# The last token tile of a cross-attention and FFN kernel in smaller pieces, with new order constants

## The chip, the cores and the metric

The kernel runs on one core of a Trainium2 chip. Its time is the device time of one execution in microseconds, and the figure used is the median over runs. A core has five engines with queues of their own: TensorE (PE, matmuls; its weight loads are shown as PEld), VectorE (DVE), ScalarE (ACT), GpSimd (POOL) and SyncE (SP, which here only issues transfers). Each queue is worked off in the order in which the program wrote it.

## The reference

There are 8 batches of 100 tokens with 512 features, and for each a context of 722 rows. Sixteen heads of 32 features attend to the context with sparsemax in place of softmax. The FFN multiplies the normalized tokens with the cosine of one matrix and the sine of another, and takes the length of the two results.

```python
def sparsemax(x):
    x = x - jnp.max(x, axis=-1, keepdims=True)
    zs = -jnp.sort(-x, axis=-1)
    rho = jnp.arange(1, L + 1, dtype=x.dtype)
    cssv = jnp.cumsum(zs, axis=-1) - 1.0
    k = jnp.maximum(jnp.sum(zs > cssv / rho, axis=-1, keepdims=True), 1)
    tau = jnp.take_along_axis(cssv, k - 1, axis=-1) / k.astype(x.dtype)
    return jnp.clip(x - tau, 0.0)

h = layernorm(x)                                     # x: (8, 100, 512)
scores = heads(h @ Wq + bq) @ heads(ctx @ Wk + bk).T * 32 ** -0.5
out = sparsemax(scores) @ heads(ctx @ Wv + bv)
x = x + merge(out) @ Wo + bo
h = layernorm(x)
real = h @ cos(theta + theta_noise)
imag = h @ sin(phi + phi_noise)
return x + sqrt(real * real + imag * imag)
```

All numbers are fp32.

## The kernel before

**Tiles.** The 800 tokens are cut into seven tiles (`TILES`: six of 128 rows and one of 32). The attention works by batch, eight of them. A tile's norm and queries come before the batches it belongs to; its last steps (output product, residual, second norm, FFN, result) follow when the last of its batches has its outputs. Tile 6, the last, holds rows 672 to 799 and so ends with batch 7; tile 5 ends with batch 6.

**A batch.** TensorE makes keys (`keys`, L559; for batch 0 also `keys_part`, L548) and values (`values`, L581) from the context. It makes the scores in ten fills of a PSUM tile of four banks, `psc` (`fill`, L606 and L617); ScalarE copies each to SBUF (`fill_copy`, L628); VectorE takes the eight largest of each stretch of some 30 scores (`tops`, L639). From these candidates the threshold of sparsemax is found in five Newton steps (`above`, `above_values`, `above_count`, `update`; L706 to L732), on VectorE with a product on POOL. POOL cuts the threshold into three bf16 parts (`parts`, L747 to L764), TensorE transposes them (`parts_T`, L769), ScalarE copies them. Then, in five groups of up to five pairs of head group and context chunk (`PAIRS`): TensorE makes the scores again less the threshold (`weights`, L813 and L826) in `psc`, ScalarE takes the relu (`weights_relu`, L838), TensorE multiplies with the values (`outputs`, L849), and after the last chunk of a head group ScalarE adds the bias into a quarter of `oT` (`outputs_bias`, L863). There is one `psc` and one `aT` buffer, so the next weights wait for the relu before, and other PE work is put between. For the last batch the threshold search is cut into three ranges of rows.

**Last steps of a tile** (`last_steps`): `product` (L502) multiplies the four quarters of `oT` with Wo; `residual` (L511) adds on VectorE; `stats`, `deviation`, `normed` (L443 to L455), `normed_T` (L463) and `normed_copy` (L469) are the norm; two more products (L502) with the cosine and sine matrices; `square` on ScalarE (L515), `square_sum` on POOL (L518), `root` on ScalarE (L521), `result` on POOL (L525), which also issues the store from POOL's queue (L526).

**The order.** No loop writes the program. Every step is a task with an engine and an assumed cost (`STEPS`), its forerunners, and the buffers it takes and frees (`hold`). `Plan.order` gives each engine, whenever it is free, the ready task that can start first, and among several the one with the smallest due time:

```python
t.due = t.batch * PERIOD - t.rank + LAG.get(t.kind, 0.0)
...
stay = STAY if engine == "PE" and t.shape == shape else 0.0
key = (max(start, now + WINDOW), t.due - stay)
```

`rank` is the longest path of costs to the end, `LAG` a constant for each kind of task, and `STAY` favours PE work of the same tiling as the work before it. A ready task is never left in order to wait for a more urgent one that isn't ready. The order found is what each engine's queue holds.

**The check.** After the planned part, VectorE reduces what `keep_checks` (L739, L740) recorded to one flag (L1190 to L1203, with a transpose on TensorE, L1199). All engines read it (L1204), and a slow general path runs if it is set; for these inputs it is not.

Of the kernel before, what the change touches and what calls it, by code (L numbers as in the profile page):

```python
# [11 lines left out]
FP = mybir.dt.float32  # L12
# [10 lines left out]
P = 128  # L23
# [12 lines left out]
FS = 16  # L36
# [7 lines left out]
def fills_of(left_first):  # L44
# [52 lines left out]
    "load ctx": ("SP", 4.8),  # L97
    "load w": ("SP", 0.8),
    "load bias": ("SP", 0.1),
    "stats": ("DVE", 0.85),  # L100
    "deviation": ("ACT", 0.25),
    "normed": ("DVE", 0.65),
# [28 lines left out]
    "values": ("PE", 3.43),  # L131
    "values copy": ("ACT", 0.55),
    "weights": ("PE", 0.05, 0.25),
    "weights relu": ("ACT", 0.12, 0.335),
    "outputs": ("PE", 0.0, 0.184),
    "outputs bias": ("ACT", 0.05, 0.28),
# [5 lines left out]
    "square sum": ("POOL", 1.25),  # L142
    "root": ("ACT", 0.6),
    "result": ("POOL", 1.9),
    "turns": ("POOL", 3.5),
    "turned": ("POOL", 2.05),
    "bounded": ("POOL", 0.7),
# [3 lines left out]

SHAPE = {"fill": 1, "fill last": 2, "outputs": 2, "weights": 3}
CHANGE = (0.19, 0.1, 0.1, 0.1)
STAY = 175.0
PERIOD = 121.0
WINDOW = 0.0
LAG = {
    "above": 260.0,
    "above count": -180.0,
    "above values": -150.0,  # L160
    "add bo": -5.0,
    "bounded": -75.0,
    "candidates": -190.0,
    "checks": 30.0,
    "deviation": 165.0,
    "ffn": 300.0,
    "fill": -240.0,
    "fill copy": 30.0,
    "fill last": -235.0,
    "first bound": 270.0,  # L170
    "keys": -65.0,
    "keys bias": 280.0,
    "keys part": -285.0,
    "leftovers": 250.0,
    "load bias": 205.0,
    "load ctx": 295.0,
    "load part": 120.0,
    "load w": 200.0,
    "load x": -160.0,
    "load x again": 180.0,  # L180
    "losses": 250.0,
    "normed": -80.0,
    "normed 2": -110.0,
    "normed T": -65.0,
    "normed copy": -245.0,
    "output product": 235.0,
    "outputs": -205.0,
    "outputs bias": 70.0,
    "parts": -180.0,
    "parts T": -165.0,  # L190
    "parts copy": -240.0,
    "parts copy last": -285.0,
    "queries": -285.0,
    "queries bias": -215.0,
    "residual": -55.0,
    "rests": 130.0,
    "result": 150.0,
    "sines": -300.0,
    "square": -215.0,
    "square sum": 275.0,  # L200
    "stats": 100.0,
    "stats 2": 265.0,
    "tops": 240.0,
    "turned": 160.0,
    "turns": -255.0,
    "update": 55.0,
    "update far": 155.0,
    "values": 110.0,
    "values copy": -200.0,
    "weights": -80.0,  # L210
    "weights relu": 300.0,
}


# [13 lines left out]
class Plan:  # L228
# [9 lines left out]
    def add(self, kind, emit, *after, tiles=1):  # L238
        t = Task(kind, emit, after, tiles)
        t.batch = self.batch  # L240
        self.tasks.append(t)
        for a in after:
            self.edge(a, t)
        return t
# [78 lines left out]
def xattn_ffn(  # L323
# [52 lines left out]
    def load_w(t, w, c):  # L376
        nc.sync.dma_start(t[:, c, :], w[c * P : (c + 1) * P, :])
# [121 lines left out]
    def product(tk, name, lhs, w_sb):  # L499
        tk[name] = ps1.tile([P, DM], FP, name="pm")[: tk["n"]]  # L500
        for c in range(NG):
            nc.tensor.matmul(  # L502
                tk[name],
                lhsT=tk[lhs][:, c, :],
                rhs=w_sb[:, c, :],
                start=(c == 0),
                stop=(c == NG - 1),
            )

    def residual(tk):  # L510
        nc.vector.tensor_tensor(tk["x"], tk["py"], tk["x"], ALU.add)  # L511
# [323 lines left out]
    def weights_relu(st, n):  # L835
        st["aT", n] = work.tile([P, HG, NP * Q], FP, name="aT", bufs=1)
        w = len(PAIRS[n]) * Q
        nc.scalar.activation(st["aT", n][:CK, :, :w], st["psw"][:CK, :, :w], AF.Relu, scale=SCALE)  # L838

    def outputs(st, n):  # L840

        aT = st.pop(("aT", n))
        for k, (g, c) in enumerate(PAIRS[n]):
            if c == 0:
                st["po", g] = ps1.tile([P, DM], FP, name="pm")
            m = min(CK, S - c * CK)
            for j in range(HG):
                f = g * P + j * HD
                nc.tensor.matmul(  # L849
                    st["po", g][j * HD : (j + 1) * HD, :Q],  # L850
                    lhsT=st["v"][:m, c, f : f + HD],
                    rhs=aT[:m, j, k * Q : (k + 1) * Q],
                    start=(c == 0),
                    stop=(c == NC - 1),
                )
# [78 lines left out]
    def last_steps(tk, outs):  # L934
# [25 lines left out]
        hold("x", xi, [rz])  # L960
        return py

    w = {}
    sines_done, turned_before = [], []
    for b in range(B):
        st, par = sts[b], b % 2
        plan.batch = b
# [3 lines left out]
        if b == 0:  # L971
            c_in, w["k"] = [], []
            for c in range(NG):
                c_in.append(add("load part", lambda st=st, b=b, c=c: load_ctx_part(st, b, c)))
                w["k"].append(add("load w", lambda c=c: load_w(wk_sb, wk, c)))
            w["bk"] = once(lambda: nc.sync.dma_start(bk_sb, bk))
            w["q"] = load_weight(wq_sb, wq)
            w["bq"] = once(lambda: nc.sync.dma_start(bq_sb, bq))
            w["bo"] = once(lambda: nc.sync.dma_start(bo_sb, bo.partition_broadcast(P)))
            w["v"] = load_weight(wv_sb, wv)  # L980
            w["bv"] = once(lambda: nc.sync.dma_start(bv_sb, bv.rearrange("(g p) -> p g", p=P)))
        else:
            c_in = [add("load ctx", lambda st=st, b=b: set_c(st, b))]
# [29 lines left out]
        for n, (pieces, _) in enumerate(st["fills"]):  # L1013
            cs = [c for c, *_ in pieces]
            if LEFT in cs:
                f = add("fill last", lambda st=st, n=n: fill(st, n), ql_in, *q_in, *ks.values())
                hold(f"ql{par}", ql_in, [f])
            else:
                gs = {divmod(HG * c + k, QB)[0] for c in cs for k in range(HG)}
                f = add(  # L1020
                    "fill", lambda st=st, n=n: fill(st, n), *q_in, *[ks[g, i] for g in gs for i in range(2)],
                    tiles=FS,
                )
            segments = FS if len(cs) == 1 or LEFT not in cs else NC3 * SEG % FS + LS
            e = add("fill copy", lambda st=st, n=n: fill_copy(st, n), f, tiles=segments)
            fills.append(f)
            hold("psc", f, [e])
            ts = [
                add("tops", lambda st=st, n=n, j=j: tops(st, n, j), e, tiles=segments)
                for j in range(HG)  # L1030
            ]
            hold("s", e, ts)
            for c in cs:
                done_tops[c] += ts
            top_steps += ts
# [4 lines left out]
        for lo, hi in ((0, HG + 1), (HG + 1, 2 * HG + 1), (2 * HG + 1, NT)) if b == B - 1 else ((0, NT),):  # L1040
# [32 lines left out]
        checks = [  # L1073
            add("checks", lambda st=st, b=b, r=r: keep_checks(st, b, **r), t, ls) for r, t in checked
        ]
        hold("l", ls, checks)
        hold("t", cds[0], [*checks, *phs, ls])
        hold("cand", top_steps[0], [*cds, ls])
# [18 lines left out]
        for n, pairs in enumerate(PAIRS):  # L1097
# [3 lines left out]
                *{t: 0 for g in gs for t in tT_of[g]}, last_rows, *q_in, *ks.values(), *ws[-1:],  # L1101
                tiles=len(pairs),
            )
            e = add("weights relu", lambda st=st, n=n: weights_relu(st, n), f, tiles=len(pairs))
            hold("psc", f, [e])
            o = add(
                "outputs", lambda st=st, n=n: outputs(st, n), e, *[vs[c] for _, c in pairs], *all_o[-1:],
                tiles=len(pairs),
            )
            hold("aT", e, [o])  # L1110
# [49 lines left out]
        for tk, at, q, n in st["out"]:  # L1160
            if "outs" not in tk:
                tk["outs"] = []
            for t in outs:
                if tk["outs"]:
                    plan.edge(tk["outs"][0], t)
                tk["outs"].append(t)
            if tk["at"] + tk["n"] <= (b + 1) * Q:
                py = last_steps(tk, tk["outs"])
                hold("oT", tk["outs"][0], [py])

        hold("c", c_in[0], [*kmm, *vmm])
        for t in c_in[1:]:
# [7 lines left out]
            plan.edge(vmm[0], t)  # L1180
        hold("tT", tT0, ws)

    with tc.manual_schedule():
        for t in plan.order():
            t.emit()

    worst = small.tile([P, 2], FP, name="worst", bufs=1)
    nc.vector.tensor_reduce(worst[:, 0:1], lost.rearrange("p b t -> p (b t)"), AX.X, ALU.max)  # L1190
    nc.vector.tensor_scalar(worst[:, 0:1], worst[:, 0:1], 0.0, None, ALU.is_gt)
    off = moved.rearrange("p b t -> p (b t)")
    nc.vector.tensor_tensor(off, off, off, ALU.mult)
    nc.vector.tensor_reduce(worst[:, 1:2], off, AX.X, ALU.max)
    nc.vector.tensor_scalar(worst[:, 1:2], worst[:, 1:2], STILL * STILL, None, ALU.is_gt)
    bad = small.tile([P, 1], FP, name="bad", bufs=1)
    nc.vector.tensor_tensor(bad, worst[:, 0:1], worst[:, 1:2], ALU.max)
    pw = ps1.tile([P, DM], FP, name="pm")
    nc.tensor.transpose(pw[:1, :P], bad, ident)  # L1199
    most = small.tile([1, 1], FP, name="most", bufs=1)  # L1200
    nc.vector.tensor_reduce(most, pw[:1, :P], AX.X, ALU.max)
    again = small.tile([1, 1], I32, name="again", bufs=1)
    nc.vector.tensor_scalar(again, most, 0.5, None, ALU.is_gt)  # L1203
    flag = nc.values_load(again[0:1, 0:1], min_val=0, max_val=1)  # L1204
    with tc.If(flag > 0):
        with tc.For_i(0, B) as b:
# [122 lines left out]
```

## Time and profile before

| | |
|---|---|
| median of 3 runs | 619.33 us (619.13 to 622.4) |
| the profiled execution | 617.21 us, span 615.6 us |
| mean granted TensorE clock | 0.994 |
| TensorE busy | 590.9 us, 96% of the span |
| VectorE busy | 520.5 us, 85% |
| ScalarE, POOL busy | 257.5 and 226.3 us |
| first matmul of the keys | 8.12 us |
| last step of the threshold search | 568.98 us |
| last product's end | 607.1 us |
| issue of the last store | 611.46 us |

A profile is of one execution, whose time is the span and 1.6 us around it. Lines of the timeline give the start, the duration, the engine, the line of the kernel, the operation, the tiles written and read with their shapes, the count, and in brackets the idle time of the engine before it with what ended it. A busy PE is not PE at its peak. The granted clock is the share of TensorE's full clock.

### The profile page before, as it was taken

How to read it: one execution, taken by the hardware profiler on the slowest of the kernel's cores; microseconds unless marked ns; L12 is line 12 of the kernel's file. 1: busy time of each engine (PE TensorE's matmuls, PEld its weight loads, DVE VectorE, ACT ScalarE, POOL GpSimd, SP SyncE). 2: the span in 40 equal slices, each digit the busy share in tenths (PEclk: the TensorE clock that was granted, in tenths of full speed). 3: DMA queues.
4: the chain of work that ended last, by engine and by line, in shares of the span. 5: the costliest groups of instructions: out<-in, count | busy, mean ns of one | idle time of the engine just before them, and what ended most of it. 6: DMA issues, size and time to landing. Idle time of an engine off the chain costs nothing.

```text
span 615.6 us, 17162 instructions
## 1 busy us (share of the span) xinstructions
PE 590.9 (96%) x6497; PEld 330.5 (54%) x6497; DVE 520.5 (85%) x3198; ACT 257.5 (42%) x355; POOL 226.3 (37%) x296
## 2 busy tenths in 40 slices
PE   5999999899999999999999999999999999999974
PEld 3755445556555655566466644675457434555531
DVE  2079999999999999997899989998999899998210
ACT  1244542355354435441644343552545334443521
POOL 1688487765500450024311650025211440165021
PEclk9999999999999999999999999999999999999998
DMA  8920012002000110002010102000030000000000
GB/s 307 364 92 19 18 56 78 18 19 98 19 2 3 40 60 2 3 2 97 19 37 2 41 2 98 3 2 1 3 132 3 0 23 2 2 20 2 2 18 21
DMA packets 12264, 26.56 MB, mean 43 GB/s; under 512 B 1856, under 2 KB 1856, under 8 KB 12176
## 3 DMA queue, kind: packets, MB, share of 16 engines
q1 hardware_dynamic: 11664, 23.77, 11.3%
q0 software_dynamic: 512, 1.64, 0.7%
q8 instruction: 53, 0.87, 0.6%
q14 instruction: 35, 0.29, 0.2%
HBM read 23.76 MB, written 1.64 MB: 41 GB/s over the span
## 4 chain that ended last, share of the span: by engine, by line
PE 46%; DVE 39%; issue 7%; POOL 5%; ACT 1%; DMA 1%; SPq 0%; POOLq 0%; DVEq 0%; ACTq 0%
DVE cand L639 19%; PE pm L581 12%; PE pm L559 12%; PE pm L502 5%; DVE f L727 4%; DVE m L706 4%; PE psc L826 3%; PE pm L849 3%; PE psc L617 3%; DVE n L717 3%; PE pm L479 3%; POOL p L711 3%; PE psc L548 2%; DVE rest L648 1%; DVE t L674 1%
## 5 line engine op out<-in xcount | busy, mean ns | idle before, releaser
L639 DVE MAX8 cand<-s_t 128x8 f32<-128x30 f32 x2496 | 230.3, 174 | 3.5 <-ACT s_t L628 3.5
L711 POOL TENSOR_TENSOR p<-z,m 128x1040 f32<-128x1040 f32 (+2 forms) x50 | 89.1, 1785 | 271.4 <-DVE m L706 269.7
L581 PE MATMUL pm<-wv_sb,c_t 128*121 128x512 f32 (+1 forms) x384 | 174.7, 600 | 0.0
L559 PE MATMUL pm<-c_t,wk_sb 128*128 128x361 f32 x464 | 150.9, 473 | 0.0
L559 PEld LDWEIGHTS pm<-c_t,wk_sb 128*128 128x128 f32 x464 | 84.5, 189 | 52.3 <-issue 7.6
L581 PEld LDWEIGHTS pm<-wv_sb,c_t 128*121 128x121 f32 (+1 forms) x384 | 67.2, 183 | 82.8 <-issue 78.3
L838 ACT ACTIVATE aT<-psc 121x2000 f32<-121x2000 f32 (+1 forms) x40 | 70.8, 1771 | 53.6 <-PE psc L826 53.6
L628 ACT COPY s_t<-psc 128x1924 f32<-128x1924 f32 (+2 forms) x40 | 69.0, 1725 | 47.9 <-DVE cand L639 23.7
L594 ACT COPY v_t<-pm 121x512 f32<-121x512 f32 (+1 forms) x48 | 28.1, 586 | 93.8 <-PE pm L581 93.8
L570 ACT ACTIVATE k_t<-pm,bk_sb 128x361 f32<-128x361 f32 x60 | 33.6, 565 | 71.1 <-PE pm L559 70.9
L727 DVE TENSOR_REDUCE f<-p 128x13 f32<-128x1040 f32 (+2 forms) x50 | 50.7, 1013 | 9.5 <-POOL p L711 9.5
L717 DVE TENSOR_REDUCE n<-m 128x13 f32<-128x1040 bf16 (+2 forms) x50 | 50.7, 1013 | 1.1
L826 PE MATMUL psc<-q_t,k_t 32*121 32x100 f32 (+1 forms) x1536 | 46.8, 262 | 0.0
L849 PEld LDWEIGHTS pm<-aT,v_t 121*32 121x32 f32 (+1 forms) x1536 | 32.7, 109 | 24.7 <-issue 21.7
L826 PEld LDWEIGHTS psc<-q_t,k_t 32*121 32x121 f32 (+1 forms) x1536 | 45.9, 180 | 0.2
L617 PE MATMUL psc<-k_t,q_t 32*32 32x481 f32 (+1 forms) x1536 | 43.2, 474 | 0.0
L849 PE MATMUL pm<-aT,v_t 121*32 121x100 f32 (+1 forms) x1536 | 41.7, 251 | 1.2 <-ACT aT L838 1.2
L479 PEld LDWEIGHTS pm<-hT,wq_sb 128*128 128x128 f32 x224 | 28.2, 191 | 8.2 <-issue 6.3
L479 PE MATMUL pm<-hT,wq_sb 128*128 128x128 f32 (+1 forms) x224 | 29.5, 277 | 0.0
L502 PE MATMUL pm<-cos_sb,hT 128*128 128x512 f32 (+1 forms) x56 | 27.5, 636 | 0.7 <-ACT hT L469 0.7
L518 POOL TENSOR_TENSOR sq<-sq 128x512 f32<-128x512 f32 (+1 forms) x7 | 8.8, 1264 | 48.7 <-ACT sq L515 48.6
L617 PEld LDWEIGHTS psc<-k_t,q_t 32*32 32x32 f32 x1536 | 13.9, 103 | 23.1 <-issue 15.4
(298 smaller groups left out, 570.9 us busy)
## 6 DMA issues: line engine op xcount, KB each, us to landing
c_t<-in_ctx SPq DMA_DIRECT2D x7, 1444.0 KB, 6.3
x_t<-in_x SPq DMA_DIRECT2D x12, 256.0 KB, 2.9
out<-sq POOLq DMA_DIRECT2D x6, 256.0 KB, 2.9
c_t<-in_ctx SPq DMA_DIRECT2D x4, 361.0 KB, 6.2
wk_sb<-in_L_xattn_Wk SPq DMA_DIRECT2D x4, 256.0 KB, 5.5
wq_sb<-in_L_xattn_Wq SPq DMA_DIRECT2D x4, 256.0 KB, 6.3
cos_sb<-in_L_ffn_theta SPq DMA_DIRECT2D x4, 256.0 KB, 3.9
n_t<-in_L_ffn_theta_noise SPq DMA_DIRECT2D x4, 256.0 KB, 3.6
```

The costliest lines, as they stand in the source:

```text
L479: nc.tensor.matmul(tk["pq"][:, g, : tk["n"]], lhsT=wq_sb[:, c, g * P : (g + 1) * P], rhs=tk["hT"][:, c, :], start=(c == 0), stop=(c == NG ...
L559: nc.tensor.matmul(pk, lhsT=wk_sb[:, c, g * P : (g + 1) * P], rhs=st["c"][:, c, i * SH : (i + 1) * SH], start=(c == 0), stop=(c == NG - 1),)
L581: nc.tensor.matmul(pv[:n], lhsT=st["c"][:, k, c * CK : c * CK + n], rhs=wv_sb[:, k, :], start=(k == 0), stop=(k == NG - 1),)
L617: nc.tensor.matmul(psc[b * HD : (b + 1) * HD, j, at : at + EDGE[hi] - EDGE[lo]], lhsT=st["q"][r, g, qb * HD : (qb + 1) * HD], rhs=st["k"][ ...
L628: nc.scalar.copy(s_t[:, :, :n], st["psc"][:, :, :n])
L639: nc.vector.max(st["cand"][:, n, k, :], st["s", f][:, j, at + EDGE[k] - first : at + EDGE[k + 1] - first],)
L711: nc.gpsimd.tensor_tensor(st["p"][:, lo:hi], st["z"][:, lo:hi], st["m"][:, lo:hi], ALU.mult)
L717: nc.vector.tensor_reduce(n_t, st["m"][:, lo:hi], AX.X, ALU.add)
L727: nc.vector.tensor_reduce(s_t, st["p"][:, lo:hi], AX.X, ALU.add)
L826: nc.tensor.matmul(psc[:m, j, k * Q : (k + 1) * Q], lhsT=st["k"][r, g, lo : lo + m], rhs=st["q"][r, g, :], start=False, stop=(k == len(PAI ...
L838: nc.scalar.activation(st["aT", n][:CK, :, :w], st["psw"][:CK, :, :w], AF.Relu, scale=SCALE)
L849: nc.tensor.matmul(st["po", g][j * HD : (j + 1) * HD, :Q], lhsT=st["v"][:m, c, f : f + HD], rhs=aT[:m, j, k * Q : (k + 1) * Q], start=(c = ...
```

## The change

For the last tile alone, `last_steps_of_all` takes the place of `last_steps`: the output product is four tasks, one for each quarter of `oT`, which accumulate in one PSUM tile; the FFN goes by halves of 256 columns (cos, sin, cos, sin), with the sum and the result on VectorE and a store from SP for each half. The relu of the last group of the last batch is cut in two, half on ScalarE and half on VectorE. The check's VectorE and TensorE operations become three tasks of the plan; reading the flag stays behind it. The weight loads of `wk` get a kind of their own. A fill that spans two chunks is given a larger assumed cost. `STAY`, `PERIOD` and all of `LAG` get other values ("normed T" and "parts copy" lose theirs, and so count as 0).

```diff
+    "load k": ("SP", 0.7),
+    "relu ACT": ("ACT", 0.12, 0.168),
+    "relu DVE": ("DVE", 0.12, 0.22),
+    "product part": ("PE", 0.86),
+    "half ffn": ("PE", 1.72),
+    "half square": ("ACT", 0.37),
+    "half sum": ("DVE", 0.4),
+    "half root": ("ACT", 0.37),
+    "half result": ("DVE", 0.4),
+    "store": ("SP", 0.6),
+    "verdict": ("DVE", 1.6),
+    "verdict T": ("PE", 0.25),
+    "verdict most": ("DVE", 0.45),
...
-STAY = 175.0
-PERIOD = 121.0
+STAY = 240.0
+PERIOD = 106.0
...
-    "ffn": 300.0,
+    "ffn": 295.0,
+    "half ffn": 125.0,
+    "load k": 225.0,
-    "load part": 120.0,
-    "load w": 200.0,
+    "load part": 185.0,
+    "load w": 220.0,
-    "normed T": -65.0,
-    "output product": 235.0,
-    "outputs": -205.0,
-    "parts T": -165.0,
+    "output product": 285.0,
+    "outputs": -135.0,
+    "parts T": 90.0,
+    "product part": 85.0,
     "values": 110.0,
-    "weights": -80.0,
-    "weights relu": 300.0,
+    "weights": -125.0,
+    "weights relu": 40.0,
...
+    def product_part(tk, name, lhs, w_sb, c):
+        if c == 0:
+            tk[name] = ps1.tile([P, DM], FP, name="pm")[: tk["n"]]
+        nc.tensor.matmul(tk[name], lhsT=tk[lhs][:, c, :], rhs=w_sb[:, c, :],
+                         start=(c == 0), stop=(c == NG - 1))
...
+    def half_ffn(tk, k, h, w_sb):
+        tk["pr", k, h] = ps1.tile([P, DM], FP, name="pm")[: tk["n"], : DM // 2]
+        for c in range(NG):
+            nc.tensor.matmul(tk["pr", k, h], lhsT=tk["hT"][:, c, :],
+                             rhs=w_sb[:, c, half_of(h)], start=(c == 0), stop=(c == NG - 1))
+    def half_square(tk, k, h):
+        if ("sq", k) not in tk:
+            tk["sq", k] = rows.tile([P, DM], FP, name="sq", tag="sq", bufs=2)[: tk["n"]]
+        nc.scalar.activation(tk["sq", k][:, half_of(h)], tk["pr", k, h], AF.Square)
+    def half_sum(tk, h):
+        a, b = (tk["sq", k][:, half_of(h)] for k in range(2))
+        nc.vector.tensor_tensor(a, a, b, ALU.add)
+    def half_root(tk, h):
+        a = tk["sq", 0][:, half_of(h)]
+        nc.scalar.activation(a, a, AF.Sqrt)
+    def half_result(tk, h):
+        a = tk["sq", 0][:, half_of(h)]
+        nc.vector.tensor_tensor(a, a, tk["x"][:, half_of(h)], ALU.add)
+    def store(tk, h, rows_of_out):
+        nc.sync.dma_start(rows_of_out[:, half_of(h)], tk["sq", 0][:, half_of(h)])
...
+    def relu_half(st, n, scalar):
+        if ("aT", n) not in st:
+            st["aT", n] = work.tile([P, HG, NP * Q], FP, name="aT", bufs=1)
+        w, j = len(PAIRS[n]) * Q, slice(0, HG // 2) if scalar else slice(HG // 2, HG)
+        a, b = st["aT", n][:CK, j, :w], st["psw"][:CK, j, :w]
+        if scalar:
+            nc.scalar.activation(a, b, AF.Relu, scale=SCALE)
+        else:
+            nc.vector.tensor_scalar(a, b, SCALE, 0.0, ALU.mult, ALU.max)
...
+        for c in range(NG):
+            parts.append(
+                add("product part", lambda c=c: product_part(tk, "py", "oT", wo_sb, c),
+                    *outs[c::NG], w["o"][c], *parts[-1:]))
...
+                if tk is tks[-1]:
+                    hold("oT", tk["outs"][0], last_steps_of_all(tk, tk["outs"]))
+                else:
+                    hold("oT", tk["outs"][0], [last_steps(tk, tk["outs"])])
...
+    vd = add("verdict", verdict, *all_checks)
+    vT = add("verdict T", verdict_T, vd)
+    hold("pm", vT, [add("verdict most", verdict_most, vT)])
```

## The prediction

> **What bounds the kernel now.** I read the busy times first, then the same by stretches, then the timeline of the last 40 us, and the waits last. The page's first two parts:
>
> ```profile
> PE 590.9 (96%) x6497; PEld 330.5 (54%) x6497; DVE 520.5 (85%) x3198; ACT 257.5 (42%) x355; POOL 226.3 (37%) x296
> ...
> PE   5999999899999999999999999999999999999974
> ...
> PEclk9999999999999999999999999999999999999998
> ```
>
> The reader is to see a TensorE that is full in every slice but the first and the last two, and a granted clock that falls only at the end. The stretches (us, then the busy time of PE, PEld, DVE, ACT, POOL, the clock, the DMA) cut this where VectorE starts and ends its search, and where the last outputs and the last product end:
>
> ```profile
> 36.00:569.00 533.00, 528.68 (x6000) 294.19 (x6002) 507.04 (x3147) 234.68 (x320) 203.04 (x253) 1.00 0.08 28
> 569.00:590.39 21.39, 19.99 (x341) 12.18 (x333) 3.23 (x11) 10.35 (x13) 1.49 (x8) 1.00 0.01 2
> 590.39:607.10 16.71, 13.11 (x33) 5.55 (x29) 2.28 (x5) 2.45 (x5) 3.12 (x3) 0.90 0.05 17
> 607.10:615.60 8.50, 0.15 (x2) 0.00 (x0) 0.42 (x2) 1.23 (x2) 3.08 (x3) 0.79 0.11 38
> ```
>
> In the middle PE is idle for 4.3 of 533 us, and VectorE for 26. So an order of the steps can win little there, and can lose much, since two engines are near full. The tail is a chain. In the timeline (start, duration, instruction, what ended the idle time before it):
>
> ```profile
> 585.94 3.70 PE L502 MATMUL pm<-sin_sb,hT 128*128 128x512 f32 x8
> 586.14 1.50 ACT L838 ACTIVATE aT<-psc 121x1600 f32<-121x1600 f32 x1 [1.21 <-PE psc L826]
> 589.57 0.90 PE L849 MATMUL pm<-aT,v_t 121*32 121x100 f32 x32
> 590.39 3.70 PE L502 MATMUL pm<-wo_sb,oT 128*128 128x512 f32 x8
> 590.53 0.34 ACT L863 ACTIVATE oT<-pm,bv_sb 128x100 f32<-128x100 f32 x1 [0.21 <-PE pm L849]
> ...
> 597.02 0.63 PE L463 MATMUL pm<-ident,h_t 128*128 128x128 f32 x4 [2.93 <-DVE h_t L455]
> ...
> 598.32 5.38 PE L502 MATMUL pm<-cos_sb,hT 128*128 128x512 f32 x8 [0.68 <-ACT hT L469]
> ...
> 603.54 3.60 PE L502 MATMUL pm<-sin_sb,hT 128*128 128x512 f32 x8
> ...
> 607.23 0.60 ACT L515 ACTIVATE sq<-pm 128x512 f32<-128x512 f32 x1 [2.83 <-PE pm L502]
> ...
> 607.91 1.25 POOL L518 TENSOR_TENSOR sq<-sq 128x512 f32<-128x512 f32 x1 [13.36 <-ACT sq L515]
> 609.20 0.63 ACT L521 ACTIVATE sq<-sq 128x512 f32<-128x512 f32 x1 [1.38 <-POOL sq L518]
> 609.90 1.26 POOL L525 TENSOR_TENSOR sq<-sq,x_t 128x512 f32<-128x512 f32 x1 [0.74 <-ACT sq L521]
> 611.46 0.56 POOL L526 DMA_DIRECT2D out<-sq  x1 [0.30 <-DVEq L1205]
> ```
>
> Three things to see. The last relu (L838) is done at 587.64, yet the outputs (L849) start at 589.57: a sin product of the tile before the last sits in front of them on PE. PE then stands still for 2.93 and 0.68 us in the norm, and the cos product after it takes 5.38 us where the others take 3.70. And 4.06 us of elementwise steps (607.10 to 611.16) lie bare behind the last product.
>
> **The change, part by part.** The profiled execution took 617.21 us (span 615.6, 1.6 around it). The median of the runs shown, 619.33, is 2.1 above it; I sum against 617.21 and carry the sum over unchanged.
>
> 1. The end of the last tile by halves. Removed: square, sum, root and result on 512 columns after the last product, 4.06 us with waits. Added: the same on 256 columns, the first half beside the products of the second, and so is the second half's cos square. Bare remain one square, sum, root and result. ScalarE: 1503 to 1838 ns for 1600 to 2000 elements is 0.84 ns an element, so 0.598 becomes 0.385 and 0.630 becomes 0.415. VectorE: its 320- and 1040-column reductions (478 and 1234 ns) give 1.05 ns an element, so the 0.676 of the 512-column add (L511) becomes about 0.41, twice. With 0.3 us of handovers: 1.94. Gain 2.1 us. The four half products are PE's same columns: 2 x 3.43 = 6.86 warm; the 361-column products cost 2.43, in proportion, so halving costs no more than 0.1. The weights are loaded twice as often; the 128-column queries (0.131 us an instruction) show that loads keep up at half that width.
>
> 2. The store goes from POOL to SP in two halves. POOL's result ends at 611.16, the span 4.44 later: 0.30 before the issue, about 2.6 to landing (median of POOL's seven stores), the rest closing. SP has no work queued then; the first half store lies ahead of the second by some 1.7 us, an issue of 0.33. [...] The row speaks against it: SP's own 256 KB loads land in 2.9 us, so the issue may even cost 0.3. Between +0.3 and -1.0 I take -0.4, nearer to the row.
>
> 3. The check in the plan. L1199 (0.27 on PE) ended beside the last square and delayed nothing; six small VectorE operations (1.0 us at 570.8) stay in a stretch where VectorE is 85% idle. Gain 0. Its new place can hurt: PE's transpose is queued behind VectorE's verdict, and whatever PE has behind it waits. No row shows this; bounds -0.1 and +1.0, I take 0, since its inputs are ready 20 us before the end.
>
> 4. The relu on two engines. 800 elements: 0.83 us on ScalarE, about 0.98 on VectorE (its PSUM add, lengthened at 1.05 ns). From 1.50 that is -0.52, but only if PE waits for it. Now 3.63 us of product cover it: 0.
>
> 5. The output product by groups. Now 3.70 us follow the outputs; after it, 0.14 + 0.34 of bias, then one part of 0.86 and a handover: 1.4. Gain 2.3. The other three parts (2.6 us) go into earlier waits for a relu. PE idles there 0.48 + 0.92 = 1.4 us, so 1.2 is pushed onto PE, and each part stands between differently tiled products: 3.63 against 3.43 shows 0.2 for such a change, so 0.6 in all. Net gain 0.5. The output product's slot in PSUM is held some 15 us longer, one of four; costed at nothing since outputs, cos and sin fit the other three, and at up to 1 us otherwise.
>
> 6. What fills the norm of the last tile. With three small parts as filler, each ranked ahead of tile 5's product and ffn (7x106 + 85 against 6x106 + 285 and + 295, less ranks of 20 and less), one of the 3.63 us products is left over, by my reading, and falls into the norm's gap. Then the outputs follow the relu: they start at 586.0 + 0.15 + 0.98 + 0.05 = 587.2, 2.4 earlier (the last part but one, 0.86, hides there). Against it: the transposes now stand behind a 3.63 us product instead of 2.93 us of idle, +0.7. Net 1.7. And PE stays at work: the cos product's extra 1.6 us (5.38, less 0.2 of closing, against 3.6) goes. [...]
>
> 7. The order constants. Everything in the middle is rearranged. What can be won there is 4.3 us of idle PE less what no order removes; what can be lost is open. The page shows no row; I take 0, with ends of -4 and +10.
>
> 8. "load k" gets a due time of its own: two due times 5 apart, at a start where each weight piece costs SP 0.33 us to issue; 0, at worst one product's wait of 1.
>
> Sum: 2.1 + 0.4 + 0.5 + 1.7 + 1.6 = 6.3. The profiled execution would be 610.9; the median 613.0.
>
> **The rivals.**
>
> A, nothing falls into the gap. The planner takes for an idle PE whatever is ready; tile 5's products are ready and go before the last outputs as now. Then steps 6 and 4 bring nothing, and PE is as cold: 2.1 + 0.4 + 0.5 = 3.0, so 616.3. For it: this is just what the trace shows at 580.17 and 585.94. Against: the parts take places that these had.
>
> B, more than that: the new order also closes the idle places of the middle. 6.3 + 4 gives 609. For it: most are single waits; against: they are few.
>
> C, slower: the new order puts each batch's threshold transposes (parts T) too early in PE's queue, which then stands behind POOL. It happens twice of eight now:
>
> ```profile
> 118.99 0.40 PE L769 MATMUL pm<-ident_b,t 128*128 128x128 bf16 x4 [2.00 <-POOL t L762]
> ...
> 367.26 0.40 PE L769 MATMUL pm<-ident_b,t 128*128 128x128 bf16 x4 [1.30 <-POOL t L762]
> ```
>
> In all eight at 2.0 us it costs 16 less the 3.3 of now, 12.7; with step 6 lost and 3.0 won, 629; with half of it, 623. It decides from 6.1 us of new waits (3.0 to eat up, 3.1 to be seen). For it: VectorE is 95% busy there, and an order written for costs that don't hold drifts. Against: six of eight transposes wait for nothing, as PE has a stock of values and products to put before them.
>
> D, the parts wait: a product part whose oT is late stands in front of weights. At 0.3 us each, 1 us: 617 to 618.5 with A, no change.
>
> **How the numbers follow.** A difference of 0.5%, 3.1 us, is about what a measurement of this kernel can tell from no change. The case of the sum, 613.0 with 610 to 615.5: 0.42, faster. A: 0.20, of which 0.09 beyond 3.1 us. B: 0.14. C: 0.18. D: 0.06, same. Faster 0.42 + 0.14 + 0.09 = 0.65; same 0.11 + 0.06 = 0.17; slower 0.18. The range goes from 606 (below the middle of B, 0.04 left out) to 623 (0.15 of C left out).
>
> **What would show it.** From the last product's end to the last store's issue about 2.0 us instead of 4.4; squares of 256 columns at 0.385 us; one product part of 0.86 behind the last bias; a product of tile 5 between that part and the transposes, and the first half products at 1.7 us, not 2.6 or more. A is right if PE shows idle times of about 2.9 and 0.7 in the last norm and a slow first half. The sum is wrong if PE's idle time between 36 us and VectorE's last search exceeds 4.3 by more than some 2 us, or if its busy time is not within 3 us of 590.9 less 1.9 of clock and check.

## The result and the profile after

The changed kernel takes 613.84 us (median of 4 runs, 613.43 to 614.25), the kernel before 619.29 beside it: a ratio of 0.9906, interval 0.9885 to 0.9928. The forecast of 613.0 and its range hold. The profiled execution took 613.43 us with a span of 611.7, so the two profiled executions differ by 3.8 us where the medians differ by 5.45; both numbers have to be explained.

The page of the changed kernel, busy times and slices, and its stretches over the windows that were read of the kernel before (busy time of PE, PEld, DVE, ACT, POOL, then the clock and the DMA):

```profile
PE 591.2 (97%) x6513; PEld 333.7 (55%) x6513; DVE 524.1 (86%) x3203; ACT 256.7 (42%) x358; POOL 221.5 (36%) x293
...
PE   5999999899999999999999999999999999999985
...
PEclk9999999999999999999999999999999999999998
```

```profile
36.00:569.00 533.00, 529.05 (x5960) 293.80 (x5962) 505.33 (x3140) 234.02 (x319) 202.69 (x256) 1.00 0.09 28
569.00:590.39 21.39, 18.74 (x375) 11.99 (x364) 7.34 (x22) 8.73 (x13) 2.28 (x9) 1.00 0.01 2
590.39:607.10 16.71, 14.22 (x52) 9.16 (x50) 3.48 (x9) 4.74 (x11) 3.12 (x3) 1.00 0.07 24
```

In the first window, the middle, PE is idle for 3.95 us, against 4.3: nothing was won there. In the third window the granted clock is 1.00 where it was 0.90. The timeline of the end shows how (SPq is an issue on SP's queue):

```profile
576.92 1.02 PE L538 MATMUL pm<-wo_sb,oT 128*128 128x512 f32 x2
578.91 1.07 PE L931 MATMUL pm<-aT,v_t 121*32 121x100 f32 x40 [0.97 <-ACT aT L909]
...
585.77 0.84 ACT L918 ACTIVATE aT<-psc 121x800 f32<-121x800 f32 x1 [1.21 <-PE psc L897]
586.64 0.99 DVE L920 TENSOR_SCALAR aT<-psc 121x800 f32<-121x800 f32 x1 [6.82 <-ACT aT L918]
...
589.01 1.13 PE L538 MATMUL pm<-wo_sb,oT 128*128 128x512 f32 x2 [0.44 <-ACT oT L945]
589.97 3.60 PE L527 MATMUL pm<-cos_sb,hT 128*128 128x512 f32 x8
...
593.40 3.60 PE L527 MATMUL pm<-sin_sb,hT 128*128 128x512 f32 x8
596.84 0.60 PE L488 MATMUL pm<-ident,h_t 128*128 128x128 f32 x4
598.21 1.99 PE L553 MATMUL pm<-cos_sb,hT 128*128 128x256 f32 x8 [0.78 <-ACT hT L494]
...
603.50 1.89 PE L553 MATMUL pm<-sin_sb,hT 128*128 128x256 f32 x8
604.18 0.38 ACT L564 ACTIVATE sq<-pm 128x256 f32<-128x256 f32 x1 [3.49 <-DMA out<-sq]
605.95 1.80 SPq L579 DMA_DIRECT2D out<-sq  x2
606.95 0.42 DVE L576 TENSOR_TENSOR sq<-sq,x_t 128x256 f32<-128x256 f32 x1 [0.48 <-ACT sq L572]
```

Four things to see. The first three parts of the output product (L538) stand in the waits for a relu. The two halves of the last relu (L918, L920) run one after the other. Behind the last part come *both* products of tile 5 (L527, 6.87 us from the first one's start), and only then the transposes (L488), for which the normalized rows had been ready since 592.92. And the result is done at 607.37, 1.98 us after the last product's end at 605.39.

To compare ends without what lies before, I take as a **mark** the start of the last batch's third weights (`3x200 bf16`, which no edit below moves): 574.26 us before, 575.42 after. From the mark to the span's end, the **tail**, is 41.34 us before and 36.28 after. The difference of the spans, 3.9 us, then splits so:

| stretch | before | after | difference |
|---|---|---|---|
| start to the mark | 574.26 | 575.42 | +1.2 |
| mark to the end of the output product | 19.83 | 14.72 | -5.1 |
| from there to the first FFN product | 4.23 | 8.07 | +3.8 |
| FFN products | 8.82 | 7.18 | -1.6 |
| last product's end to the result | 4.02 | 1.98 | -2.0 |
| result to the span's end | 4.44 | 4.33 | -0.1 |

### The profile page after: what moved, and what is told of

Its sections match the earlier page's. It is cut to its first block, busy times and chain, and to the rows that moved or that the text cites. A ratio compares the mean times of both kernels' runs of the same rounds, so it can differ in the third digit from the quotient of the medians.

```text
span 611.7 us, 17204 instructions
## 1 busy us (share of the span) xinstructions
PE 591.2 (97%) x6513; PEld 333.7 (55%) x6513; DVE 524.1 (86%) x3203; ACT 256.7 (42%) x358; POOL 221.5 (36%) x293
## 4 chain that ended last, share of the span: by engine, by line
PE 66%; DVE 24%; issue 5%; ACT 2%; POOL 1%; DMA 1%; SPq 0%; POOLq 0%; ACTq 0%; DVEq 0%
PE pm L630 18%; PE pm L652 16%; DVE cand L710 11%; PE pm L527 7%; PE psc L688 5%; PE psc L897 5%; PE pm L931 5%; PE pm L504 3%; DVE m L777 2%; DVE f L798 2%; PE psc L619 2%; DVE n L788 2%; PE psc L884 2%; PE psc L677 1%; DMA wk_sb<-in_L_xattn_Wk 1%
## 5 line engine op out<-in xcount | busy, mean ns | idle before, releaser
L909 ACT ACTIVATE aT<-psc 121x2000 f32<-121x2000 f32 (+1 forms) x39 | 69.3, 1778 | 57.7 <-PE psc L897 57.7
L688 PE MATMUL psc<-k_t,q_t 32*32 32x481 f32 (+1 forms) x1536 | 44.1, 474 | 1.2 <-ACT s_t L699 1.2
L527 PE MATMUL pm<-cos_sb,hT 128*128 128x512 f32 (+1 forms) x48 | 22.0, 601 | 0.0
```

Source lines behind the costliest of these rows:

```text
L527: nc.tensor.matmul(tk[name], lhsT=tk[lhs][:, c, :], rhs=w_sb[:, c, :], start=(c == 0), stop=(c == NG - 1),)
L688: nc.tensor.matmul(psc[b * HD : (b + 1) * HD, j, at : at + EDGE[hi] - EDGE[lo]], lhsT=st["q"][r, g, qb * HD : (qb + 1) * HD], rhs=st["k"][ ...
```

## Experiments

**The changed kernel again** (no edit), as the control for the next three.

> The changed kernel once more, as the measure for what follows: about 613.8 us, PE idle in the tail (569 us to its last product) about 3.4 us, cos product of the last tile at full clock. Theory T (TensorE's tail): the gain is a shorter end behind the last product (2.0 us), the clock that stays up (1.7) and less idle PE in the tail (5.0 to 3.4), less some 2 us that the new order costs elsewhere. Theory R (order): the new constants bring the gain in the whole kernel, the pieces little.

612.98 us against 619.74, ratio 0.9896 (0.9873 to 0.9919); tail 36.31. From the second batch's threshold transposes to the mark it took 406.49 us, as in the first profile to the hundredth. Nine changed kernels have 406.46 to 406.66 there; only the stretch up to those transposes varies (167.06 to 170.87), and single spans vary with it. Tails and medians are therefore given side by side.

**The end whole.** The FFN, squares, sum, root and result of the last tile on 512 columns again, sum, result and store on POOL, in the same places of the order.

```diff
-  "half ffn", lambda k=k, h=h, w_sb=w_sb: half_ffn(tk, k, h, w_sb)
+  "half ffn", lambda k=k, h=h, w_sb=w_sb: h or product(tk, ("pr", k), "hT", w_sb)
-  "half sum", lambda h=h: half_sum(tk, h)
+  "half sum", lambda h=h: h or square_sum(tk)
...
-  lambda h=h: store(tk, h, ...)
+  lambda h=h: None
```

> The changed kernel, its order untouched, with the end of the last tile as before: whole cos and sin product, 512 columns for square, sum (POOL), root, result (POOL), one store from POOL. T: the bare end behind the last product grows from 2.1 to about 4.1 us and the store by 0.1: plus 2.1, 615.9 us (615.4 to 616.4). R: below plus 1, up to 614.8, since the halves only shift work.

615.18 us, ratio 0.9927 (0.9906 to 0.9948): 2.2 us slower than the control, and the tail 38.08, 1.8 longer. Timeline of this kernel:

```profile
603.54 0.60 ACT L586 ACTIVATE sq<-pm 128x512 f32<-128x512 f32 x1 [2.83 <-PEq L1356]
604.23 1.25 POOL L589 TENSOR_TENSOR sq<-sq 128x512 f32<-128x512 f32 x1 [4.20 <-ACT sq L586]
605.51 0.63 ACT L592 ACTIVATE sq<-sq 128x512 f32<-128x512 f32 x1 [1.37 <-POOL sq L589]
606.22 1.26 POOL L596 TENSOR_TENSOR sq<-sq,x_t 128x512 f32<-128x512 f32 x1 [0.74 <-ACT sq L592]
607.78 0.56 POOL L597 DMA_DIRECT2D out<-sq  x1 [0.30 <-POOL sq L596]
```

The chain from the square to the result is 3.94 us, the one of before (3.93). Step 1 of the prediction is shown. The result is done at 607.48 and the span ends 4.12 later, no later than with SP's store (4.33, 4.43): the queue of the store brings nothing.

**The parts late.** The first three parts of the output product directly in front of the fourth; all else as changed.

```diff
+        pps = pick("product part", B - 1)
+        move(pps[:-1], pps[-1], 0)
```

> The changed kernel with the first three parts of the last output product moved behind the last outputs, in front of the fourth; cos and sin of the tile before stay in the norm's gap. T: the parts no longer fill the waits for the relu: PE idle in the tail grows from 3.4 to about 5.9, the clock stays up: plus 2.5, 616.3 us. Rival R2 (the parts pay for themselves on PE, each with a change of tiling): about the same, within 0.7 of the changed kernel.

618.27 us, ratio 0.9987 (0.9972 to 1.0001): 5.3 slower than the control, twice what was expected, and tail 40.06, 3.75 longer. Timeline:

```profile
577.43 1.07 PE L931 MATMUL pm<-aT,v_t 121*32 121x100 f32 x40 [1.83 <-ACT aT L909]
...
581.94 1.07 PE L931 MATMUL pm<-aT,v_t 121*32 121x100 f32 x40 [1.44 <-ACT aT L909]
...
585.18 0.37 PE L931 MATMUL pm<-aT,v_t 121*32 121x100 f32 x4 [1.03 <-ACT aT L918]
586.20 0.88 PE L931 MATMUL pm<-aT,v_t 121*32 121x100 f32 x28 [0.66 <-DVE aT L920]
587.02 5.40 PE L538 MATMUL pm<-wo_sb,oT 128*128 128x512 f32 x8
```

The waits now add to 4.96 us, against 2.65 with the parts between (0.97, 0.58, 0.66, 0.44): 2.3 as expected. The other part is the product itself, 5.40 for 3.70: the granted clock was 0.50 from 587.09 to 590.50, after waits of 1.83, 1.44, 1.03 and 0.66 us with matmuls between them. In the changed kernel it is 1.00 from 569.00 to the last product's end. So here the parts fill the waits *and* keep the clock up. The medians' further 1.5 us lie in no part of the two profiles, but they go with the clock. The profiled execution had a mean granted clock of 0.992; of the 22 executions, the eight with 0.992 or more have a median of 616.9 us, the fourteen with less (down to 0.981) of 619.2. The ten executions of the changed kernel in the result and the control all had 0.995 to 0.998.

**The gap open.** In addition, tile 5's two products in front of the last outputs, so that nothing fills the last norm, as before.

```diff
+        move(pps[:-1], pps[-1], 0)
+        move(ffn, outs[-1], 0)      # tile 5's cos and sin
+        move(sq, outs[-1], 0)
```

> As the kernel with the parts late, and the cos and sin product of the tile before also moved: from the last norm's gap to in front of the last outputs. T: the gap of 3.6 us stands open again and the clock falls (1.6); the wait for the last relu is filled instead (1.6): about plus 2.8 against the kernel with the parts late, plus 5.3 against the changed kernel, 619 us; the first half products at half speed. Rival R2: the products delayed the transposes by 3.9 us in the gap, so with the gap open the norm runs at once and nothing is lost: within 1 us of the kernel with the parts late, at 616 to 617.

621.0 us, ratio 1.0016 (0.9999 to 1.0032): 2.7 slower than the parts late, where 2.8 was expected if filling the gap pays, and 8.0 slower than the control. Timeline:

```profile
586.38 3.70 PE L527 MATMUL pm<-cos_sb,hT 128*128 128x512 f32 x8
...
600.81 0.66 PE L488 MATMUL pm<-ident,h_t 128*128 128x128 f32 x4 [2.84 <-DVE h_t L480]
...
602.19 3.59 PE L553 MATMUL pm<-cos_sb,hT 128*128 128x256 f32 x8 [0.73 <-ACT hT L494]
```

Idle times of 2.84 and 0.73 are back, and with them a first half product of 3.59 us instead of 1.99 (granted clock 0.67 from 600.81 to 605.58). The tails of the two profiles differ by only 0.8 (40.86 to 40.06), since each had one slow product. The sign and size of the medians stand; that they come from the gap alone is not shown by these profiles.

**The new constants alone**: the kernel before with the new `STAY`, `PERIOD` and `LAG`. (The opposite, the new structure with the old constants, gives the planner no startable task and was not run.)

```diff
-STAY = 175.0
-PERIOD = 121.0
+STAY = 240.0
+PERIOD = 106.0
 LAG = { ... }   # the changed kernel's values, for the kinds that exist
```

> The kernel before with nothing changed but STAY, PERIOD and LAG. T: the new order costs some 2 us on PE in the middle (search end 2.8 us later in the changed kernel's profile, other PE work 2.0 us longer) and cannot close the last norm's gap, since no product part holds a PSUM slot there: 0 to plus 3 against before, 619.7 to 622.7 us; the last cos product is slow (about 5.4 us) as before. R: the constants bring the gain: 613 to 616 us.

620.79 us against 618.97, ratio 1.0021 (1.0004 to 1.0038). The constants by themselves bring nothing. In this profile the start up to the second batch's threshold transposes took 171.89 us, against 168.80 to 169.65 in the three profiles with before's constants and order (the first, and two below). Timeline:

```profile
599.66 1.09 PE L461 MATMUL pm<-ident,h_t 128*128 128x128 f32 x4 [2.93 <-DVE h_t L453]
```

The last norm's gap is as wide as before. It is closed by the new tasks, then, not by the constants alone.

**The last relu on one engine.**

```diff
-  lambda st=st, n=n, k=k: relu_half(st, n, k)
+  lambda st=st, n=n, k=k: k and weights_relu(st, n)
```

> The changed kernel with the last relu whole on ScalarE, order untouched. In the changed kernel's profile VectorE's half started only when ScalarE's half was done: 0.84 + 0.99 = 1.87 us. T: the split costs 0.3: the outputs' second part starts about 0.35 us earlier, the end 0.3 earlier (within the noise of the times; the trace decides). Rival: the halves overlap in most executions and the split saves 0.5: the end comes 0.5 later.

613.55 us, ratio 0.9904 (0.9874 to 0.9935), not to be told from the control; tail 36.00, 0.3 shorter. Timeline:

```profile
585.75 1.50 ACT L909 ACTIVATE aT<-psc 121x1600 f32<-121x1600 f32 x1 [1.21 <-PE psc L897]
...
587.30 0.90 PE L931 MATMUL pm<-aT,v_t 121*32 121x100 f32 x32 [0.64 <-ACT aT L909]
```

Whole, the relu is done at 587.25, 11.85 us from the mark; by halves it was at 587.63, 12.21 from the mark. The outputs on the second half waited for that.

**The halves with separate outputs**, to see what makes VectorE wait: its half goes into an `s_t` tile. With it, the squares of the last tile get storage of their own (the free `p` and `z` of the search), since a square of the first half waited 3.49 us for tile 5's store.

```diff
+            st["a2"] = work.tile([P, HG, FW], FP, name="s_t", bufs=2)
+            a = st["a2"][:CK, : HG // 2, :w]
...
-  tk["sq", k] = rows.tile([P, DM], FP, name="sq", tag="sq", bufs=2)[: tk["n"]]
+  tk["sq", k] = work.tile([P, NT, CAND], FP, name="pz"[k], bufs=1)...
```

> The changed kernel with VectorE's half of the last relu in a tile of its own, and the last tile's squares in tiles of their own (storage that is free by then), order untouched. If the wait of VectorE for ScalarE comes from the shared tile, both halves run side by side and the outputs follow 0.85 us earlier; if it comes from reading the same PSUM tile, nothing moves. The squares no longer wait for the store of the tile before (3.5 us in the changed kernel): the first half's chain ends 3 us earlier, the last by 0.3. Sum: minus 0.3 to minus 1.1 us.

612.55 us, ratio 0.99 (0.9875 to 0.9925); tail 36.15, 0.15 shorter. Timeline:

```profile
585.77 0.99 DVE L924 TENSOR_SCALAR s_t<-psc 121x800 f32<-121x800 f32 x1 [6.82 <-ACT aT L922]
...
602.88 3.80 SPq L579 DMA_DIRECT2D out<-p  x2
```

VectorE still starts only after ScalarE, so the shared output tile isn't the cause. What is left is that both read one PSUM tile, `psc`; two PSUM tiles were not tried. The order stands in the program itself: VectorE's half waits there for the count of ScalarE's semaphore (341) that ScalarE's half raises. So it says nothing on whether the two engines could read side by side. From the mark, the first half's result is done 2.2 us earlier than in the changed kernel, and the end moves by only 0.15: the second half sets it.

**The transposes first**: the last norm's transposes and their copy between tile 5's cos and sin products, with `hT` in the free storage of the mask, as its own buffer is still read by the sin product.

```diff
+        sin = pick("ffn", B - 2)[-1]
+        move(pick("normed T", B - 1)[-1:], sin, 0)
+        move(pick("normed copy", B - 1)[-1:], pick("square", B - 2)[-2], 1)
```

> The changed kernel with the transposes of the last norm moved in front of the sin product of the tile before (second buffer for hT). T: PE has no idle time in the gap either way, only the 0.78 us before the first half product goes: the end 0.8 earlier. Rival R2: the 3.9 us for which the transposes stand behind both products are lost time: the end 3 us or more earlier.

613.04 us, ratio 0.9902 (0.9873 to 0.9931); tail 36.66, 0.35 longer. Timeline:

```profile
602.95 0.38 ACT L567 ACTIVATE sq<-pm 128x256 f32<-128x256 f32 x1 [4.28 <-PEq L1373]
```

Measured from the mark PE is done 1.0 us earlier, and the next square is not: ScalarE stood still until 602.95. The releaser that the row names, PE, had long been done; but the last tile's squares take over tile 5's `sq` buffers, and tile 5's store was issued only at 600.03. In the next kernel, where the squares have storage of their own, the wait is gone. A store that was hidden had become the bound.

**The three together**: relu on one engine, squares in storage of their own, transposes first.

> The changed kernel with three mends of its tail, order otherwise untouched: the last relu whole on ScalarE, the last tile's squares in tiles of their own, the transposes of the last norm in front of the sin product of the tile before. T: from the third weights of the last batch to the end 36.3 us become about 34.6: 0.3 from the relu, 1.1 that the earlier transposes give on PE (seen as PE's last product 1.1 earlier, given back since the squares then waited for a store), 0.3 from the squares: minus 1.7, about 611.5 us. Rival: the end then hangs on the store of the tile before, and half of it is lost: 612.5.

Tail 34.66 against 36.31, 1.6 shorter, as expected from the parts. The time is 612.71 us, ratio 0.9894 (0.9879 to 0.9909): shorter than the kernel before, and not to be told from the changed kernel. In its profile the start up to the second batch's transposes took 170.87, 2.2 more than the control's.

**The old order with the new end.** Before's order, with the last steps of the changed kernel and the three mends put in by hand.

```diff
+  work.tile([P, NG, P], FP, name="h2", tag="m", bufs=1) if tk is tks[-1] and tk.get("late")
...
+        last["late"] = True      # set before anything is written
+        put([cos5, rs, st2, dev, sqc, nm2, nT, sin5, nC, sqs, *rest5], parts_[3])
```

> The kernel before with its own order constants and its order up to the last weights; only the tail is laid by hand as in the mended changed kernel (product parts behind weights 3 to 5, cos product, transposes and sin product in the last norm's gap, FFN by halves, SP stores). T: the new constants only cost in the middle (1.8 us when put alone on the kernel before), so this is faster than the mended changed kernel by 1 to 2: 609.5 to 611 us. R: without the constants the gain shrinks: 614 or more.

629.68 us, ratio 1.0162 (1.0145 to 1.0178): a miss, by an error of mine. The flag holds for the last tile's *first* norm as well, which then also sits in the mask's storage. A row of this kernel's waits, between the threshold transposes of the fifth and sixth batch:

```profile
DVE m L755 <- PE pm L482: 17.9, 1, 17.9
```

The search waits once for 17.9 us, until the queries have read it. The end itself was as planned (tail 35.56), but the time says nothing on the old order.

**Before, profiled again** (no edit), and **before, kept warm**: three matmuls into a PSUM tile that nobody reads, behind the last output product, where PE stood still for 2.93 us.

```diff
+        def warm():
+            idle = ps1.tile([P, DM], FP, name="pm")
+            for c in range(3):
+                nc.tensor.matmul(idle, lhsT=tk5["hT"][:, c, :], rhs=sin_sb[:, c, :], ...)
```

> The kernel before again, for a second profile: how its tail differs between executions. T: up to the third weights it comes within 2 us of the first profile, all of the difference arising in the first 170 us, and the slow clock in the last FFN costs between 1.6 and 2.5, depending on when the clock falls; the total 618 to 621 us.

> The kernel before with three matmuls of 512 columns (2.6 us, a result that nothing reads) behind the last output product, so that PE works through most of the last norm's gap. Nothing else moves. T: the clock stays up, the last cos product takes 3.6 to 3.7 us instead of 5.4: minus 1.6 against before, about 617.7. Rival: the slow product is not the clock but a cold weight load or a wait on hT: no change, 619.3.

Again: 619.31 us, ratio 1.0006 (0.9989 to 1.0022). Kept warm: 617.82, ratio 0.9975 (0.996 to 0.9989), 1.5 us less with work added. Timeline of before, profiled again, then of before, kept warm:

```profile
596.55 0.88 PE L463 MATMUL pm<-ident,h_t 128*128 128x128 f32 x4 [2.93 <-DVE h_t L455]
...
598.10 6.42 PE L502 MATMUL pm<-cos_sb,hT 128*128 128x512 f32 x8 [0.68 <-ACT hT L469]
```

```profile
594.75 2.74 PE L1191 MATMUL pm<-sin_sb,hT 128*128 128x512 f32 x6
597.75 0.66 PE L463 MATMUL pm<-ident,h_t 128*128 128x128 f32 x4 [0.26 <-DVE h_t L455]
599.08 3.70 PE L502 MATMUL pm<-cos_sb,hT 128*128 128x512 f32 x8 [0.67 <-ACT hT L469]
```

The idle place, not the data or the tiling, slowed the cos product, and by 1.7 to 2.7 us (5.38 and 6.42 for 3.70). The second profile of before also shows that the first was a favourable one: the tail is 44.11, not 41.34. Of the 2.77 us, 1.3 are the transposes and the cos product (0.88 and 6.42, for 0.63 and 5.38), and 1.5 the last store. DMA issues of the last stretch, before profiled again:

```profile
out<-sq POOLq DMA_DIRECT2D x1, 256.0 KB, 4.1
```

It lands after 4.1 us; in the first profile of before after 2.6. Result to span's end is 4.44 us there, but 5.9 here, 6.2 kept warm and 6.0 with the new constants. In the nine kernels that have the changed order it is 4.1 to 4.5, the one that stores from POOL among them.

**Where the clock fell.** Stretches of the parts late, then of before, profiled again (the length of the stretch, then PE's busy time; the granted clock is the third number from the end):

```profile
580.26:583.68 3.42, 1.98 (x70) 1.59 (x69) 0.00 (x0) 2.45 (x3) 0.00 (x0) 1.00 0.02 5
583.68:587.09 3.41, 1.72 (x53) 1.18 (x45) 0.99 (x1) 0.84 (x1) 0.00 (x0) 1.00 0.00 0
587.09:590.50 3.41, 3.41 (x4) 1.38 (x5) 0.00 (x0) 0.34 (x1) 0.00 (x0) 0.50 0.00 0
590.50:593.92 3.42, 3.42 (x9) 1.52 (x8) 1.40 (x3) 0.00 (x0) 0.00 (x0) 1.00 0.00 0
```

```profile
593.38:596.79 3.41, 0.48 (x3) 0.27 (x3) 2.28 (x5) 0.29 (x1) 0.59 (x1) 1.00 0.20 77
596.79:600.20 3.41, 2.73 (x7) 1.30 (x6) 0.00 (x0) 0.58 (x1) 0.00 (x0) 0.50 0.02 5
600.20:603.62 3.42, 3.42 (x5) 1.35 (x5) 0.00 (x0) 0.00 (x0) 0.00 (x0) 0.50 0.00 0
603.62:607.03 3.41, 3.41 (x9) 1.50 (x9) 0.00 (x0) 0.60 (x1) 0.00 (x0) 1.00 0.00 0
```

With the parts late, the clock stayed at 1.00 behind the 3.42 us that hold 1.44 us of idle PE (580.26 to 583.68). It was 0.50 for the 3.41 us behind those that hold 1.69 (583.68 to 587.09, with the waits of 1.03 and 0.66), and 1.00 again behind 3.41 us of busy PE. In before, profiled again, it was 0.50 for 6.83 us (596.79 to 603.62) behind 3.41 us with 2.93 of idle PE; the first half of the 6.83 holds 0.68 us of idle PE, the second none. With the new constants the transposes and the cos product of that place took 1.09 and 5.81 us. In the first profile of before the clock was 0.50 only from 598.33 to 601.74, behind 3.42 us with 2.79 of idle PE. Why the same kernel has 3.41 us of half clock in one profile and 6.83 in another was not shown. In the changed kernel the clock is 1.00 from the mark to the last product's end, with 3.43 of those 29.97 us idle on PE (waits of 0.97, 0.58, 0.66, 0.44 and 0.78).

Part of the varying start goes with the clock, too: in before, profiled again, and in before, kept warm, the first batch's threshold transposes wait 2.00 us; the product behind them took 4.34 us in one and 2.65 in the other, and in the slice there, the eighth of 40, the pages have the clock at 8 and 9 tenths. In the changed kernel's first profile they wait 2.51 us, and the product behind them took 4.07 at a clock of 0.50 (120.48 to 123.90).

## Why the prediction came out right, and where it did not

The forecast for the profiled execution was 610.9 us, and it took 613.43: of the predicted 6.3 us the profiles show 3.8. The median came within a us of 613.0 in part by luck: the profile that I summed against was a short one. What the change removes, the slow cos product and the store's long landing, costs 2.8 us more in the second profile of before, and from that profile the changed one is 6.2 us better (617.9 to 611.7). Carrying a sum over from one execution to the median "unchanged" was an error that went my way.

1. *The end by halves*, -2.1. Right: -2.0 in the profile, undone +1.8 in the tail and +2.2 in the median.
2. *The store to SP*, -0.4. No run shows this term, nor the 1.0 at the end of its range: the profiles show -0.1, and with the store left on POOL the end is no later, so SP brings nothing. The row, SP's own 256 KB loads that land in 2.9 us, was the better guide. But of the four profiles with before's end, three take some 1.5 us more from the result on than the first, and none with the changed order does. What the nine have in common is that the check has left the end. The old order with the new end keeps the check there and stores from SP; it takes 5.2, more than any of the nine. That speaks for the check, but nothing was run with the check alone moved, so the cause is open.
3. *The check in the plan*, 0. Right: its transpose took 0.27 us at 576.81, and PE did not wait for it.
4. *The relu on two engines*, "0, covered". The cover went, as step 6 foresaw, and the 0.98 us that step 6 reckons for the relu stands for two halves side by side. They take 0.84 and 0.99 in turn, 1.86 in all, against 1.50 whole: a loss of 0.36 instead of a gain of 0.52. I had assumed two engines side by side without a row that shows it.
5. and 6. *The product by groups and what fills the gap*, together -2.2. Relative to the mark the first FFN product starts 1.3 earlier (-5.1 and +3.8). Two terms of the sum were wrong. The parts do more than fill waits: moved back with nothing in their place they cost 3.75 in the tail and 5.3 in the median, because they also keep the clock up (1.00 with them, 0.50 for 3.41 us without), which step 5 does not count. (That is no measure of its 0.5, as in the kernel before tile 5's products stood in those waits.) And the gap got not "one of the 3.63 us products" but both, so the transposes came 3.9 us after their input. The reason is the term of step 5 that I "costed at nothing": the PSUM slot. Read from the kernel's own plan, tile 5's products are ready at 576.15 of the plan's time but get a `pm` slot at 584.08, since the one of the four that comes free next is held by the unfinished output product; and the transposes, ready at 586.43, wait until 591.14 for tile 5's sin product to free the one `hT` buffer. With another `hT`, and moved by hand, the transposes ran 0.48 us behind their input (591.24 to 591.72 in that profile); a fifth slot was not tried.
6. *The clock*, -1.6. Right: the FFN products take 1.6 less. In the first profile of before the clock was 0.50 for 3.41 us there; in its second it was for 6.83, and the cos product took 6.42. The kernel before, kept warm, shows the same with three matmuls added and nothing else changed: 3.70 for the cos product. How much idle time it takes these runs do not settle: the product behind waits of 1.03 and 0.66 us took 5.40 (the parts late), the one at 586.38, behind waits of 1.83 and 1.44, took 3.70 (the gap open).
7. *The order constants*, 0. From the second batch's threshold transposes to the mark the changed kernel takes 406.49 us, before 405.46 (404.57 and 405.43 in its two later profiles): a loss of 1 to 2. With the constants alone it is 404.89, so they don't cause it by themselves.
8. *Load k*, 0. The start varies by more than it could bring.

Rival A fell on the two products in the gap, B on 3.95 us of idle PE in the middle, C on the middle's loss of 1 to 2 where it needed 6.1. Of D, only the last part waited, 0.44, and what it waits for is the end of the chain itself.

## What to carry to other kernels

A product whose inputs come in pieces can be cut along its contraction and used as filler; ask then how long its PSUM slot is held and which ready work that keeps off the engine. When filler is put into a gap, look at what stands behind the filler: here two products fitted where one was wanted, and moving the transposes past one of them only exposed a store, until the buffer that waited for it was changed as well. Filler paid twice here, since it also kept the clock up: without it the clock was 0.50 for 3.41 us, and a product of 3.70 us took 5.40. So read the granted clock of the stretch behind the waits as well as the waits. And take the cost of an end from more than one profile: the same code's tail measured 41.3 and 44.1 us.

## What the runs showed that was not expected

- With the parts late, waits of 1.03 and 0.66 us stood in front of a product that took 5.40 us for 3.70, at a granted clock of 0.50 for 3.41 us. A slow product behind the last norm's gap cost from 1.6 us (the gap open, 3.59 for 1.99) to 2.7 (before, profiled again, 6.42 for 3.70), and in two profiles the transposes before it were slow as well (0.88 and 1.09 us, 0.63 otherwise).
- Adding 2.7 us of useless matmuls in an idle place made the kernel 1.5 us faster.
- ScalarE and VectorE, each reading its half of one PSUM tile, ran one after the other (0.84 us, then 0.99), also with separate outputs: the program that was built had a wait between them.
- The same 256 KB store from POOL landed after 2.6 us in one profile of the kernel before and after 4.1 us in another.
